# Image 1's queries and offset convolution between image 0's gathers

## The chip, the cores and the metric

The kernel runs on one core of one Trainium2 chip. The metric is the device time of one execution in microseconds (us); smaller is better. The core's engines are called PE (matrix products), DVE, ACT and POOL (work on vectors), and SP (only transfers); each takes its instructions from its own queue in order, and DMA transfers run beside them, issued by SP, ACT or POOL. "PE clock" is the share of full speed granted to PE, as the profile records it.

## The reference

Four layers stand one after another, each `x = x + f(gn(x))`, where `gn` is a group norm of 32 groups; x is [4, 32, 32, 384] in float32. Layer 0, a deformable attention of six heads, is what matters here (B images, n = 1024 pixels, G = 6 groups of GC = 64 channels):

```python
q = jnp.einsum('bhwc,cd->bhwd', x, w_q) + b_q
o = lax.conv_general_dilated(q, w_off0, ..., feature_group_count=G) + b_off0   # 3x3
o = layer_norm(o) * ln_g + ln_b;  o = gelu(o)
offset = tanh(einsum(o per group, w_offp)) * [H/2, W/2]
pos = offset + ref                                   # where each pixel of each group samples
xs = _bilinear_sample(xg, pos)                       # four neighbours of pos, weighed
k = xs @ w_k + b_k;  v = xs @ w_v + b_v
attn = softmax(q k^T * scale + _bilinear_sample(rpe, (ref - pos) / 2))
out = (attn @ v) @ w_out + b_out
```

Layer 1 is a grouped attention with 12 heads of 32 channels, which begins with the products `x @ Wg` and `x @ Wqkv`; layer 2 is a normalised box sum; layer 3 is a local attention over 3 x 3 patches.

## The kernel before

**Two lanes.** `Front` computes layer 0 of an image and `Trunk` its layers 1 to 3. The trunk of image b needs the output of front b. Image 0's front therefore runs alone, `layer0(0)`, some 520 us. From then on `layer3` steps the trunk of image b as a generator, and after each step it draws steps of the fronts of images 1 to 3 (`self.fronts`) until the share of front work that has been issued is ahead of the trunk's by LEAD: `TRUNK_STEPS, FRONT_STEPS, LEAD = 1109.0, 714.0, 0.1`. The numbers that a generator yields are its estimates of the work. The order in which the program issues instructions is the order on each engine's queue but for a scheduler, which may move an instruction ahead of others that it doesn't depend on; `keep_in_program_order` (called `pin`) forbids that for the instructions given to it. Tiles come from pools; a tile with a tag and `bufs` buffers waits, at the next use of a buffer, until the readers of its last use are done. A pool has a side, left or right, and goes out of use at the end of its scope; the next pool takes the memory.

**Layer 0 of one image.** Channels are kept in KC = 3 tiles of P = 128 partitions, pixels in NJ = 8 tiles.

- `normed(b)` loads the image in eight pieces (a<-in_x), transposes it to channels on partitions (PE, L589), writes it to DRAM (`x0`), and takes the group norm: `stats` (two bn_stats and a bn_aggr for each third, L324), a mean over groups by a product with `gmat` (L358), and one scaling for each third (L382). It then transposes the result back (L612), copies it to a tile `xn` with ACT (L624), and stores each piece twice to the DRAM table `pairs` (L626, SP), from which the gathers read. For image 1 `xn` has two buffers.
- `inputs0(b)`: queries, for each of the three output tiles one `dense_t` of six 128 x 512 matmuls in float32, which a trace shows as two records each (L403), put into the zero-framed `qpad` by ACT and stored to `q0` by SP (L660). Then the offset convolution, 36 matmuls of 64 x 64 for each of three tiles (L676), evicted by ACT to `oT` (L684). Transposes (L697) and copies (L701) bring it to pixels on partitions. The layer norm, GELU, and `positions` (L500 to L569: sampling positions, bilinear weights `w4`, pixel indices `sidx` and window indices `widx`) run in two halves for image 0.
- Gathers: for each pixel tile j six indirect DMAs issued by POOL (L748, `gat`, three buffers), 48 in all. `weigh(j)` multiplies and adds them on DVE (L761 to L764) to a tile `xs` of the tag `xn` (two buffers), `turn(j)` transposes that on PE (L775) and copies it with ACT (L780) to `xsT`, and for image 0 `value(j)` makes six matmuls of 128 x 384 (L417) and an addition on DVE (L792). The loop issues gather(j+2), turn(j-1), weigh(j), value(j-2). When all are done, the keys follow (18 matmuls through `dense_t`, L403; L818, L819).
- Heads: `heads0` for image 0 works through 96 blocks of 128 x 512 in a software pipeline of its own. POOL gathers a window of the position bias (L999, L1131, from `strips`), `z` and `lg` are made by DVE and ACT, PE adds the bias by a product with diagonal matrices `dg` (L1052, L1058) and multiplies by keys and values. `outputs0` is the output projection, with the residual, to DRAM (`x1`).

**What image 0's front does for image 1.** In the heads of image 0, `early0` runs `normed(1)` in small steps, one between blocks. The normalised image 1 goes to DRAM (`xh1`, L636). In image 1's own `inputs0`, the first thing that the trunk's first loop draws from `self.fronts`, it is loaded again by ACT's queue (L645, a<-xh) and the queries and convolution follow.

**Start of the trunk.** `start()` (L1190) loads image 0's x1 in three chunks (whole<-x) on SP, takes the norm (L324, L358, L382), and its first product is Wg (L403, big<-whole), then Wqkv.

Of the kernel before, what the change touches and what calls it, by code (L numbers as in the profile page):

```python
# [26 lines left out]
P = 128  # L27
# [34 lines left out]
TRUNK_STEPS, FRONT_STEPS, LEAD = 1109.0, 714.0, 0.1  # L62
# [10 lines left out]
class Net:  # L73
# [135 lines left out]
    def scratch(self):  # L209

        self.pairs = []
        for i in range(2):
            t = self.dram.tile([G * SLOTS, 2 * GC], F32, tag=f"pairs{i}", name=f"pairs{i}")
            self.pairs.append(t)
        dram = lambda name, shape: self.dram.tile(shape, F32, tag=name, name=name)

        self.x0 = [dram(f"x0_{i}", [C, N]) for i in range(2)]
        self.x1 = [dram(f"x1_{i}", [C, N]) for i in range(2)]

        self.qd, self.kd, self.xgd, self.yd = (dram(n, [C, N]) for n in ("qd", "kd", "xgd", "yd"))  # L220

        self.xh1 = dram("xh1", [C, N])
        self.q0, self.k0 = dram("q0", [C, N]), dram("k0", [C, N])
        self.gcd = dram("gcd", [C, M1])
        self.vd = dram("vd", [N, C])

        self.nd, self.rnd = dram("nd", [NH1, N + M1]), dram("rnd", [NH1, N + M1])

        self.den = [dram(f"den{h}", [1, N]) for h in range(G)]
        self.rden = [dram(f"rden{h}", [1, N]) for h in range(G)]  # L230
        self.lse = [dram(f"lse{p}", [2, N]) for p in range(NH1 // 2)]
        self.skew = [
            self.dram.tile([NJ, P * ROWP], F32, tag=f"skew{i}", name=f"skew{i}")
            for i in range(2)
        ]
# [39 lines left out]
    def layer0(self, b):  # L275

        if b == 0:
            for _ in self.front.layer0(b):
                pass
            self.done = self.ahead = 0.0  # L280
            self.fronts = (w for i in range(1, NB) for w in self.front.layer0(i))
# [7 lines left out]
    def layer3(self, b, out):  # L289

        for w in self.trunk.image(b, out):
            self.done += w / TRUNK_STEPS
            while self.ahead < self.done + LEAD:
                self.ahead += next(self.fronts, FRONT_STEPS) / FRONT_STEPS
        assert self.ahead >= min(b + 1, NB - 1)
# [130 lines left out]
class Front(Lane):  # L426


    def layer0(self, b):
        nc, v = self.nc, self.nc.vector  # L430
        with self.scope("l0"):
            self.qpad = self.wt([P, KC, PW, PW], "qpad")
            nc.gpsimd.memset(self.qpad, 0.0)
# [8 lines left out]
            if b == 0:  # L442

                self.side = "left"
                with self.scope("l0f"):
                    self.side = "right"
                    self.heads = self.heads0(self.work)
                    with self.scope("l0a"):
                        yield from self.inputs0(b)
                    yield from self.heads  # L450
                    self.side = "left"
                    yield from self.outputs0(b)
                    self.side = "right"
                return
# [35 lines left out]
    def positions(self, oall, js, tmp, w4, sidx):  # L490
# [37 lines left out]
        floor(fl, qc, HW)  # L528
        v.tensor_tensor(al, q, fl, ALU.subtract)
# [12 lines left out]
        fi = self.wt([P, len(js), G], "ix_fi")  # L542
        fi2 = fi.rearrange("p j g -> p (j g)")

        def index(out, hi, lo, mul, which):
            v.scalar_tensor_tensor(fi2, hi, float(mul), lo, ALU.mult, ALU.add)
            v.tensor_tensor(fi, fi, bc(self.gofs[:, which, :], 1, len(js)), ALU.add)
            v.tensor_copy(out, fi2)

        index(sidx[:, cols], fl[:, 1, :], fl[:, 0, :], HW, 0)  # L550

# [78 lines left out]
    def early0(self):  # L632

        with self.scope("l0p"):
            xh = yield from self.normed(1)
            self.nc.sync.dma_start(self.xh1.rearrange("(k p) n -> p k n", p=P), xh)  # L636

    def inputs0(self, b):
        nc, v = self.nc, self.nc.vector
        pairs = self.pairs[b % 2]  # L640
        if b == 1:

            xh = self.wt([P, KC, N], "a12", 2)
            for k in range(KC):
                nc.scalar.dma_start(xh[:, k], self.xh1[k * P : (k + 1) * P, :])  # L645
            yield 25
        else:
            xh = yield from self.normed(b)
        yield 10
        qpad = self.qpad  # L650
        w = self.weights("w_q")
        for ko in range(KC):
            ps = self.dense_t(w, xh, ko)
            nc.scalar.activation(
                qpad[:, ko, 1 : 1 + HW, 1 : 1 + HW],
                ps.rearrange("p (y x) -> p y x", y=HW),
                AF.Identity,
                bias=self.col(C_BQ, ko),
            )
            nc.sync.dma_start(  # L660
                self.q0[ko * P : (ko + 1) * P, :].rearrange("c (y x) -> c y x", y=HW),
                qpad[:, ko, 1 : 1 + HW, 1 : 1 + HW],
            )
            yield 5


        oT = self.wt([P, KC, 2, N // 2], "a12", 2)
        for k in range(KC):
            ps = self.big().rearrange("p (g n) -> p g n", g=2)
            woff = self.conv_weights(k)  # L670
            for t in range(9):
                dy, dx = divmod(t, 3)
                for h in range(2):
                    for g in range(2):
                        ch = slice(GC * g, GC * (g + 1))
                        nc.tensor.matmul(  # L676
                            ps[GC * h : GC * (h + 1), g, :],
                            woff[ch, t, ch],
                            qpad[ch, k, dy + 16 * h : dy + 16 * h + 16, dx : dx + HW],
                            start=t == 0,  # L680
                            stop=t == 8,
                        )
            for g in range(2):
                nc.scalar.activation(  # L684
                    oT[:, k, g, :], ps[:, g, :], AF.Identity, bias=self.boff[:, k, g : g + 1]
                )
            yield 15
        if b == 0:
            self.cut()
# [16 lines left out]

        parts = 2 if b == 0 else 1
# [4 lines left out]
        for part in range(parts):  # L712
            js = range(size * part, size * (part + 1))
            for j in js:
                st = self.wt([P, 6], "ln_st", 2)
                v.bn_stats(st, oall[:, j, :])
                v.bn_aggr(mv[:, j, :], st)
            rstd = self.wt([P, size], "ln_rstd", 2)
            nc.scalar.activation(
                rstd,  # L720
                mv[:, js.start : js.stop, 1:2].rearrange("p j o -> p (j o)"),
                AF.Sqrt,
                bias=self.eps[:, 1:2],
            )
            v.reciprocal(rstd, rstd)
            for i, j in enumerate(js):
                o = oall[:, j, :]
                v.scalar_tensor_tensor(
                    o, o, mv[:, j, 0:1], self.rows[:, R_LNG : R_LNG + C], ALU.subtract, ALU.mult
                )  # L730
                v.scalar_tensor_tensor(
                    o, o, rstd[:, i : i + 1], self.rows[:, R_LNB : R_LNB + C], ALU.mult, ALU.add
                )
            for j in js:
                nc.scalar.activation(oall[:, j, :], oall[:, j, :], AF.Gelu)
            yield 25 / parts
            self.positions(oall, js, tmp, w4, sidx)
            yield 20 / parts
# [5 lines left out]
        def gather(j):  # L744
            gat = self.wt([P, G, 2, 2 * GC], "gat", 3)
            for g in range(G):

                nc.gpsimd.indirect_dma_start(  # L748
                    out=gat[:, g].rearrange("p l c -> p (l c)"),
                    out_offset=None,  # L750
                    in_=pairs[:, :],
                    in_offset=bass.IndirectOffsetOnAxis(
                        ap=sidx[:, j * G + g : j * G + g + 1], axis=0
                    ),
                )
            return gat

        def weigh(j, gat):
# [5 lines left out]
            v.tensor_tensor(  # L764
# [4 lines left out]
            )  # L769
            return xs  # L770
# [15 lines left out]
        gats, xss = {0: gather(0), 1: gather(1)}, {}  # L786
# [13 lines left out]
        for j in range(NJ + 1):  # L800
# [4 lines left out]
            if j < NJ:  # L805
                xss[j] = weigh(j, gats.pop(j))
            if b == 0 and j > 1:
                value(j - 2)
            if j > 0:
                yield 7  # L810
        if b == 0:

# [129 lines left out]
    def heads0(self, work):  # L942
# [13 lines left out]

        def tile_of(shape, tag, bufs):
            return work.tile(shape, F32, tag=tag, name=self.nm(tag), bufs=bufs)
# [31 lines left out]
        def turn(t):  # L990
# [5 lines left out]
            if i + 5 < n:  # L996
                h, q, j = blocks[i + 5]
                win[i + 5] = tile_of([P, (HH + 1) * WROW], "win", 6)
                nc.gpsimd.indirect_dma_start(  # L999
# [6 lines left out]
                )  # L1006
# [120 lines left out]

        for i in range(4):
            h, q, j = blocks[i]
            win[i] = tile_of([P, (HH + 1) * WROW], "win", 6)  # L1130
            nc.gpsimd.indirect_dma_start(  # L1131
# [6 lines left out]
            )  # L1138
# [5 lines left out]
        other = self.early0()  # L1144
        for t in range(-3, n + OUT + 12):
            turn(t)
            if t > 2 * NJ:
                next(other, None)
        yield 0

    def over_sums(self, k):
# [20 lines left out]
        yield 2  # L1172

# [836 lines left out]
```

## Time and profile before

| What | us |
|---|---|
| runs shown, before (three) | 4414.36, 4414.2, 4400.94 |
| median of them | 4414.2 |
| the profiled execution, its own time | 4398.5 |
| its span, first to last instruction | 4396.7 |
| PE busy in the span | 3905.3 (89%), granted clock 0.949 |
| DVE busy | 3107.1 (71%) |
| ACT busy | 2307.2 (52%) |
| POOL busy | 955.4 (22%) |

The durations come from the profiled execution, whose time includes 1.8 us beside the span (4398.5 - 4396.7). The busy shares are means over a front in which one image is alone and a trunk in which two generators share the engines, so the front is best read by its stretches. Image 0's front, by the trace: normed, queries and convolution from 0 to 78 us; layer norm and positions to 107; gathers, weighing and values to 177; keys to 199; heads to 480; output projection to 517; the trunk's first product is at 573.5.

### The profile page before, as it was taken

The page shows a single profiled execution, that of the slowest core. Times are in us where ns is not written, and L with a number is a line of the kernel's source. Part 1 is how long each engine was busy: PE and PEld are TensorE (multiplying, and loading weights), DVE is VectorE, ACT ScalarE, POOL GpSimd, SP SyncE. Part 2 cuts the span into 40 slices and gives each one's busy share as a digit, 9 for nine tenths or more (in the row PEclk, how much of TensorE's full clock was granted, in tenths as well). Part 3 has the DMA queues.
Part 4 walks back from the last instruction along what each step waited for, and adds up shares of the span by engine and source line. Part 5 has one row for each costly group of instructions (what it writes and reads, how often), then busy time and mean ns, then how long its engine had stood idle before and what let it go on. Part 6 is the DMA issues. An engine that isn't in the chain of part 4 may idle for free.

```text
span 4396.7 us, 45258 instructions
## 1 busy us (share of the span) xinstructions
PE 3905.3 (89%) x14792; PEld 1673.4 (38%) x14792; DVE 3107.1 (71%) x5897; ACT 2307.2 (52%) x3641; POOL 955.4 (22%) x975
## 2 busy tenths in 40 slices
PE   5588889998999898999899989888989998999998
PEld 2233334333334343333333444343333344344444
DVE  4599565888887638687878754768787874566654
ACT  2177343766665324566666433456675741566633
POOL 0655223212212104211212010522121311000000
PEclk8799989999999998999999999899999999999999
DMA  7445244222212255312322135432121213311111
GB/s 149 161 148 146 94 123 139 86 59 75 68 54 68 74 159 164 106 53 56 88 59 85 39 100 159 146 110 67 46 86 41 84 36 128 115 34 34 32 33 43
DMA packets 299052, 389.73 MB, mean 89 GB/s; under 512 B 168694, under 2 KB 230402, under 8 KB 298818
## 3 DMA queue, kind: packets, MB, share of 16 engines
q1 hardware_dynamic: 246130, 220.14, 18.1%
q0 software_dynamic: 39936, 145.53, 10.9%
q10 hardware_dynamic: 12752, 21.19, 1.5%
q8 instruction: 117, 1.92, 0.2%
q14 instruction: 117, 0.96, 0.1%
HBM read 300.48 MB, written 86.56 MB: 88 GB/s over the span
## 4 chain that ended last, share of the span: by engine, by line
PE 49%; DVE 24%; issue 9%; ACT 9%; POOL 4%; DMA 4%; SPq 0%; ACTq 0%; DVEq 0%; POOLq 0%
PE bank L1586 10%; PE big L1556 6%; PE big L403 5%; DVE nmax L1430 4%; DVE e L1593 3%; PE bank L925 3%; ACT big L1431 3%; PE bank L417 3%; PE big L1421 3%; POOL gat L748 3%; PE bank L1581 2%; PE big L676 2%; PE bank L1259 2%; PE bank L1528 2%; PE bank L890 2%
## 5 line engine op out<-in xcount | busy, mean ns | idle before, releaser
L1586 PE MATMUL bank<-whole,sg 128*128 128x512 f32 (+3 forms) x2304 | 850.4, 500 | 2.1 <-POOL sg L1539 0.6
L1593 DVE SCALAR_TENSOR_TENSOR e<-bank,gam,e 128x512 f32<-128x512 f32 x768 | 560.3, 747 | 294.9 <-PE bank L1586 175.5
L1431 ACT ACTIVATE big<-big,nmax 128x1024 f32<-128x1024 f32 x384 | 417.4, 1087 | 295.9 <-DVE nmax L1430 295.8
L1586 PEld LDWEIGHTS bank<-whole,sg 128*128 128x128 f32 x2304 | 399.5, 196 | 348.0 <-issue 269.7
L1556 PE MATMUL big<-qa,ka 64*128 64x512 f32 x1536 | 445.2, 661 | 87.1 <-ACT big L1431 83.6
L1430 DVE TENSOR_REDUCE nmax<-big 128x1 f32<-128x1024 f32 x384 | 452.7, 1218 | 60.7 <-PE big L1421 60.5
L1564 ACT ACTIVATE e<-big 128x1024 f32<-128x1024 f32 x384 | 381.7, 1019 | 172.8 <-PE big L1556 162.0
L866 POOL DMA_INDIRECT win<-strips,widx x288 | 313.6, 1089 | 692.1 <-DVE z L879 377.5
L1539 POOL TENSOR_SCALAR sg<-whole,gam 128x512 f32<-128x512 f32 x192 | 150.2, 782 | 1336.3 <-PE bank L1586 1070.0
L1421 PE MATMUL big<-k,q 32*128 32x512 f32 x1536 | 270.1, 655 | 46.2 <-ACT big L1431 33.7
L748 POOL DMA_INDIRECT gat<-pairs,sidx x192 | 211.0, 1099 | 363.9 <-DVE ix_gt L520 212.2
L925 PE MATMUL bank<-lg,va 128*128 128x512 f32 x576 | 267.3, 605 | 14.7 <-ACT lg L924 14.7
L1556 PEld LDWEIGHTS big<-qa,ka 64*128 64x128 f32 x1536 | 145.8, 196 | 344.7 <-ACT big L1431 178.6
L884 DVE SCALAR_TENSOR_TENSOR lg<-z,bias_f,lg 128x512 f32<-128x512 f32 x288 | 216.2, 768 | 47.4 <-ACT lg L883 45.6
L878 ACT ACTIVATE z<-win,bias_f 128x528 f32<-128x528 f32 x288 | 205.3, 736 | 56.1 <-DVE lg L884 26.2
L923 DVE TENSOR_TENSOR lg<-lg,tb 128x512 f32<-128x512 f32 x288 | 182.2, 691 | 73.0 <-ACT tb L916 73.0
L879 DVE SCALAR_TENSOR_TENSOR z<-win,bias_f,z 128x528 f32<-128x528 f32 x288 | 215.5, 765 | 20.0 <-ACT z L878 18.4
L1528 PE MATMUL bank<-e,vs 128*32 128x512 f32 x1536 | 212.0, 621 | 17.1 <-DVE vs L1522 17.1
L1598 ACT COPY gn<-bank 128x128 f32<-128x128 f32 (+2 forms) x288 | 106.1, 369 | 204.9 <-DVE e L1593 203.9
L883 ACT ACTIVATE lg<-z,bias_f 128x512 f32<-128x512 f32 x288 | 199.7, 716 | 15.3 <-DVE z L879 12.4
L893 DVE TENSOR_TENSOR lg<-bank,lg 128x512 f32<-128x512 f32 x288 | 191.4, 683 | 12.2 <-PE bank L890 11.4
L890 PE MATMUL bank<-qs,kz 64*128 64x512 f32 x288 | 169.0, 671 | 13.4 <-DVE e L1593 8.3
(311 smaller groups left out, 6297.7 us busy)
## 6 DMA issues: line engine op xcount, KB each, us to landing
q<-qd SPq DMA_DIRECT2D x48, 256.0 KB
xg<-xgd SPq DMA_DIRECT2D x48, 256.0 KB
w<-in_gmat SPq DMA_DIRECT2D x16, 576.0 KB
pairs<-gat SPq DMA_DIRECT2D x48, 192.0 KB
w<-in_w_off SPq DMA_DIRECT2D x12, 576.0 KB
w<-in_Wqkv SPq DMA_DIRECT2D x12, 576.0 KB
a<-in_x SPq DMA_DIRECT2D x16, 384.0 KB
x<-a ACTq DMA_DIRECT2D x4, 1536.0 KB
```

What stands on the lines that cost most here:

```text
L748: nc.gpsimd.indirect_dma_start(out=gat[:, g].rearrange("p l c -> p (l c)"), out_offset=None, in_=pairs[:, :], in_offset=bass.IndirectOffse ...
L866: nc.gpsimd.indirect_dma_start(out=win, out_offset=None, in_=self.strips[:, :], in_offset=bass.IndirectOffsetOnAxis(ap=self.widx[:, q, c : ...
L890: nc.tensor.matmul(ps[u], w, mov, start=True, stop=True)
L925: nc.tensor.matmul(po, self.values_of(h, j), lf, start=j == 0, stop=j == NJ - 1)
L1421: nc.tensor.matmul(ps[r][:, h * 512 : (h + 1) * 512], self.q4[rows, i * P : (i + 1) * P], self.k4[rows, 0:512], start=True, stop=True,)
L1430: v.tensor_reduce(nmax[:, r, i : i + 1], ps[r], AX.X, ALU.max, negate=True)
L1431: nc.scalar.activation(ps[r], ps[r], AF.Exp, bias=nmax[:, r, i : i + 1], accum_out=den[:, r, i : i + 1],)
L1528: nc.tensor.matmul(av[r0 : r0 + HD1, :], vs[:, r, :], es[h][:, r, :], start=j == 0, stop=j == NJ - 1,)
L1556: nc.tensor.matmul(ps[:, r, :], ka[rows, j * P : (j + 1) * P], qa[rows, cols], start=True, stop=True,)
L1564: nc.scalar.activation(e, ps, AF.Exp)
L1586: last = nc.tensor.matmul(ps[:, (mid - i0) * P :], sg[:, r, m, :], sim[:, h, r, m, (mid - i0) * P :], start=m == 0, stop=m == 1,)
L1593: v.scalar_tensor_tensor(e[:, r, :], ps, self.gam[:, 1:2], e[:, r, :], ALU.add, ALU.mult, accum_out=tot[:, r, h : h + 1],)
```

## The change

Image 1's queries and offset convolution are computed by a new generator, `Early`, between the parts of image 0's `inputs0`, ahead of image 0's heads, together with image 1's `normed`. `EARLY = (12, 0, 14, 8, 8)` says how many of its steps are taken: 12 ahead of image 0's layer norm, none after its first half, 14 after its second half, 8 in the first round of the loop over gathers and 8 in each later round; what is left runs ahead of the keys. `early0` goes. The padded queries (`qp1`, 1.78 MB) and the convolution (`of1`, 1.57 MB) of image 1 go to DRAM in place of `xh1` (1.57 MB), and image 1's `inputs0` loads them instead of computing them; it still stores `q0` for its heads. Image 1 needs no memset of `qpad` there. Early's weights are in a pool of their own with two buffers.

Beside that: the gathers and the windows' gathers are pinned to the program's order; each `weigh` is kept behind the one before (`issue_after`); the first half of image 0's layer norm and positions is issued with high priority; `positions` computes the pixel index `sidx` ahead of the bilinear weights and not after them (all images); the pools of `heads0` are split in two (`l0f` for win, z and dg, `l0g` for the rest), and the second, with the first four windows, is opened after the inputs, where Early's memory has come free. The windows' first four gathers are thus issued after all 48 gathers. FRONT_STEPS becomes one number for each image, all 714 as before.

```diff
-TRUNK_STEPS, FRONT_STEPS, LEAD = 1109.0, 714.0, 0.1
+EARLY = (12, 0, 14, 8, 8)
+TRUNK_STEPS, FRONT_STEPS, LEAD = 1109.0, (714.0, 714.0, 714.0), 0.1
...
+                    self.heads = self.heads0(room)
+                    next(self.heads)
+                    self.early = Early(self.net, "left").begin(b + 1)
                     with self.scope("l0a"):
                         yield from self.inputs0(b)
                     yield from self.heads
...
+        index(sidx[:, cols], fl[:, 1, :], fl[:, 0, :], HW, 0)
         v.tensor_tensor(al, q, fl, ALU.subtract)
...
         if b == 1:
-            xh = self.wt([P, KC, N], "a12", 2)
-            for k in range(KC):
-                nc.scalar.dma_start(xh[:, k], self.xh1[k * P : (k + 1) * P, :])
-            yield 25
+            nc.sync.dma_start(qpad.rearrange("p k y x -> p (k y x)"), self.qp1)
+            oT = self.wt([P, KC, 2, N // 2], "a12", 2)
+            nc.scalar.dma_start(oT.rearrange("p k g n -> p (k g n)"), self.of1)
+            yield 95
...
+        for _ in range(EARLY[0]):
+            next(ahead, None)
         parts = 2 if b == 0 else 1
...
+                if b == 0 and part == 0:
+                    stack.enter_context(self.tc.high_priority())
...
+            for _ in range(EARLY[1 + part]):
+                next(ahead, None)
...
-                nc.gpsimd.indirect_dma_start(
+                pin(nc.gpsimd.indirect_dma_start(
...
-                xss[j] = weigh(j, gats.pop(j))
+                with ExitStack() as stack:
+                    if weighed:
+                        stack.enter_context(self.tc.issue_after(weighed[-1]))
+                    xss[j] = weigh(j, gats.pop(j))
             if b == 0 and j > 1:
                 value(j - 2)
+            for _ in range(EARLY[-2 + (j > 0)]):
+                next(ahead, None)
...
+            for _ in ahead:
+                pass
             next(self.heads)
...
-        other = self.early0()
         for t in range(-3, n + OUT + 12):
             turn(t)
-            if t > 2 * NJ:
-                next(other, None)
...
+class Early(Front):
+    def weights(self, name, lo=0):
+        return Net.weights(self, name, lo)
+    def conv_weights(self, k):
+        return self.taps[k] if k in self.taps else Net.conv_weights(self, k)
+    def norm_steps(self, x, out):
+        gmat, self.wq = self.weights("gmat"), self.weights("w_q")
+        yield from super().norm_steps(x, out, None, gmat)
+        self.taps = {}
+        self.taps[0] = self.conv_weights(0)
+    def begin(self, b):
+        nc = self.nc
+        with self.scope("l0p"), self.tc.tile_pool(
+            name=self.nm("l0w"), bufs=2, side=self.side
+        ) as self.wts:
+            self.qpad = self.wt([P, KC, PW, PW], "qpad")
+            nc.gpsimd.memset(self.qpad, 0.0)
+            xh = yield from self.normed(b)
+            for ko in range(KC):
+                self.project(xh, ko, self.wq)
+                yield
+            self.taps[1] = self.conv_weights(1)
+            oT = self.wt([P, KC, 2, N // 2], "a12", 2)
+            for k in range(KC):
+                yield from self.convolve(oT, k)
+            nc.sync.dma_start(self.qp1, self.qpad.rearrange("p k y x -> p (k y x)"))
+            nc.sync.dma_start(self.of1, oT.rearrange("p k g n -> p (k g n)"))
```

`project` and `convolve` are the loops of `inputs0` for the queries and the convolution, taken out into functions; `convolve` yields after each tap (9 for each tile).

## The prediction

> **What bounds the kernel now.** I read the page first (PE busy 89% of the span, but about half in the first two of its 40 slices), then busy time by stretches of the first 760 us, then the timeline of the places where PE idles, then the chain of waits there. The change touches only image 0's solo front and the start of the trunk.
>
> First the solo front, busy time by stretches (columns: stretch, then busy us and instructions of each engine, granted clock, DMA share, GB/s):
>
> ```profile
> core 0: us, PE busy (x) PEld busy (x) DVE busy (x) ACT busy (x) POOL busy (x), PEclk, DMA share, GB/s
> 90.00:95.00 5.00, 0.00 (x0) 0.00 (x0) 5.00 (x7) 1.20 (x3) 0.00 (x0) 0.50 0.00 0
> 160.00:170.00 10.00, 5.81 (x12) 3.38 (x13) 4.29 (x5) 0.48 (x1) 7.73 (x8) 0.66 0.33 97
> 240.00:260.00 20.00, 18.59 (x51) 7.28 (x51) 19.93 (x27) 14.98 (x25) 11.10 (x12) 1.00 0.34 101
> 340.00:360.00 20.00, 16.91 (x54) 7.03 (x54) 17.45 (x26) 11.87 (x23) 9.53 (x10) 1.00 0.90 246
> 520.00:530.00 10.00, 1.87 (x3) 0.81 (x4) 4.05 (x11) 1.28 (x1) 0.16 (x2) 0.54 0.90 322
> ```
>
> Layer norm and positions (78 to 107) are DVE alone. The gathers (107 to 177) are POOL's: one issue every 1.25 us, PE half idle. The heads (199 to 480) are DVE's, at 19.9 of 20 us, except in 340 to 380, where image 1's early work makes ACT wait for its stores (6.8 us in two waits, below) and DVE idles 2.55 and 1.49 us.
>
> Then the hand-over to the trunk: the timeline of PE, the transfers and DVE, the chain of waits (start, us, what), and the longest wait of that early work in 240 to 370.
>
> ```profile
> 186.68 10.46 PE L403 MATMUL big<-a,w 128*128 128x512 f32 x24
> 198.92 1.45 PE L1052 MATMUL big<-z,dg 128*128 128x512 f32 x3
> ...
> 528.13 2.04 PE L403 MATMUL big<-a,w 128*128 128x512 f32 x2 [11.14 <-DMA a<-xh]
> 529.97 2.99 PE L358 MATMUL bank<-gn_mv,w 128*128 128x2 f32 x14
> 532.82 17.38 PE L403 MATMUL big<-a,w 128*128 128x512 f32 x34
> 550.13 23.41 PE L676 MATMUL big<-qpad,w 64*64 64x512 f32 x216
> ```
> ```profile
> 522.40 0.32 SPq L1190 DMA_DIRECT2D whole<-x  x1
> 522.62 1.31 ACTq L645 DMA_DIRECT2D a<-xh  x3
> 527.67 1.29 DVE L324 BATCH_NORM_STATS2 gn_st<-whole 128x6 f32<-128x512 f32 x2 [5.38 <-DMA whole<-x]
> 534.12 2.26 DVE L382 TENSOR_SCALAR whole<-whole,gn_mean,gn_rstd 128x1024 f32<-128x1024 f32 x3
> ```
> ```profile
> 550.20 23.34 PE big L676 x216
> 573.54 10.50 PE big L403 x24
> ```
> ```profile
> ACT xn L624 <- DMA pairs<-xn: 6.8, 2, 5.1
> ```
>
> This is the heart of the case. The trunk's input is normalised by 536.4 (534.12 + 2.26), but its first product, Wg at 573.5, stands in PE's queue behind image 1's queries (to 550) and offset convolution (to 573.5). DVE and ACT, idle from 536 to 580 but for evictions, wait with it. The chain of waits runs through all of it.
>
> **The change, part by part.** By the compiled order of the instructions on each engine (which has no times), from Wg on, PE's order is the same to the end; DVE's and POOL's differ by neighbours changing places.
>
> Trunk start. Leave the 18 query and 108 convolution matmuls out, and Wg waits for its own input: statistics done, mean product L358, 534.12 the scaling, PE at about 535.2. That is 573.5 - 535.2 = 38.3 us less. Two things take some back.
> (a) In the after, SP issues the load of the padded queries (1.78 MB) ahead of the trunk's last input chunk (0.52 MB), and ACT the convolution's load (1.57 MB) beside it, where before the weights (0.59) and xh (1.57) ran. At the 322 GB/s of the row 520 to 530, split evenly between the two queues from 522.6: some 1 MB of queries left plus the chunk is 1.5 MB at 160 GB/s, 9.4 us, so it lands near 533 and not 527.7: +5.5. Bounds: 0 if the chunk gets through at once, +8 if all is served first (3.9 MB, 12 us, behind 2 us of latency that both have).
> (b) A cold clock: 36 query pieces took 2.04 + 17.38 = 19.4 us at 0.54 and 0.60, Wg's 24 10.57 at 1.00, so 15.9 for 36: the start cost 3.5, and Wg now pays it. Bounds 2 to 5.
> By the Trainium skill ("TensorE: Matmul & The Clock Gate", Part 1: The HAM clock gate), PE runs at half rate after an idle window of some 3.4 us and until a busy one has passed; by that the cold start would lose 1.7 us a window, and (b) would be 1.7 to 3.4. The trace's 0.50 at idle agrees.
> The query stores (3, of 2.9 us of SP each at 48 us) now stand together on SP at about 531 to 540, ahead of the second Wqkv weights; PE needs those 24 us after Wg begins, so 10 us and more of cover. ACT loses 3 x 1.12 + 6 x 0.63 = 7 us here, off the path: nothing. Sum: -38.3 + 5.5 + 3.5 = -29.3.
>
> Heads. Out go 6 bn_stats (3.98 us), 3 aggregates (0.59), 3 scalings (2.85) and 5 small DVE rows (0.16 each): 8.2 us of an engine that is full, and the 3.9 us that it idled in 340 to 380. I take -11 (bounds -8, if other waits fill the idle, and -13). PE's 55 and ACT's 16 smaller pieces are not on the path.
>
> Layer norm, ahead of the first gather. The same statistics (3.98 + 0.59 + 0.65 for four small rows) now lie in DVE's full stretch: +5.2; the mean product, 3.1 us on PE, is covered by about 2 us of L500 and casts: +1.2; some seven of image 1's first transposes (2.80 us for 12) precede the first eviction that DVE needs: +1.6; about 8 small rows of 0.1 us move behind the pixel index: -0.8. First gather at 114.6, not 107.4. SP and DMA: image 1's weights and first chunk (1.6 MB) go out before SP's stores to pairs, in 25 to 35 us where the DMA share is 0.48 and 0.41; nothing, and up to +5 if the third convolution weights, for which PE already waits 2.97 us at 65.7, land later. The strips, pushed behind three loads, are due only at the windows, which POOL now issues 40 us later.
>
> Gathers and keys, by two paths. POOL: 52 issues (four of them windows) took 107.4 to 177.0, 1.34 us each; now 48, so the last leaves at 114.6 + 64.3 = 178.9; the windows after it still precede the z that waits for the last turn. With the 21.9 us that lay between last gather and L1052, and 14 key matmuls instead of 12 behind the last turn (+1.7), that path ends at 202.5. PE: from the first scaled third of image 1 (about 119) until L1052 it must now do image 1's last 24 transposes (0.27 each, 6.5), queries (15.9 warm, see (b)) and convolution (23.4) beside its own turns (24 at 0.27, 6.5), values (8 at 2.10) and keys (36 pieces, 10.46 for 24: 15.7): 84.8 us, so 203.8; with one cold start of 3.5 and about 1 us for the second convolution weights, which SP sends behind image 1's stores, 208.3. PE is the later: it becomes the bound of this stretch, and image 0's values and turns, which stand in its queue behind image 1's work, and DVE's next weigh behind each value, come late by 4 to 7 us on the way. I take 208.3, +9.4 on 198.9. Bounds: +3.6 (POOL's path) and +25 (PE cold in half of its new work). The stores of image 1 go through two buffers; eight copies took 331.8 to 358.5, 27 us, and here some 30 lie open. The two last stores (3.35 MB, 10 us at 322) go out by 180, under the keys; the heads' tiles that reuse that memory are first written near 190.
>
> Images 1 to 3: their pixel index is written about 1 us earlier and the chain passes through POOL's gathers after 629; I take -1.5 in all (0 to -3). Pinning the gathers leaves their order: nothing.
>
> Total: -29.3 - 11 + 9.4 - 1.5 = -32 us. Against the profiled execution's own 4398.5 that is 4366, against the median of the runs shown, 4414.2, it is 4382. Two of the three runs lie at the median and one, at 4400.9, with the profile, so I take 4411 for the kernel before and give 4379. All low ends together make -36.3 - 13 + 3.6 - 3 = -49, all high ones -25.3 - 8 + 25 + 0 = -8: the forecast's own range is 4350 (-49 on 4398.5, were the next runs like the profile) to 4403 (-8 on 4411), and 4408 with the 5 us of the convolution weights.
>
> **A rule that speaks against it.** The row is the chunk's 5.27 us from issue (522.40) to use. By the Trainium skill ("DMA: Bandwidth & Descriptors", Queues, rings and completion order) each DMA engine goes round-robin over the queue rows, and within one row descriptors start in ring order, so a small load behind a large one on SP waits for it; that is what (a) prices, and without it the sum would be 5.5 us lower. The row cannot tell the two queues apart.
>
> **Rivals.**
> 1. The opened gap is refilled: Wg does not go when its input lands, or what follows (image 1's norm and taps share DVE, full in 590 to 620; its gathers are on the chain at 630) has a limit that does not move with Wg. For it: PE idles 12 us in 620 to 660 even now. Against: all of that follows Wg or loads that now come earlier. Then only heads and front count, -11 + 9.4, and a fifth of the trunk's 29 (-6): -8, 4403.
> 2. Slower: image 1's stores choke the gathers. ACT's third copy waits for the stores of its first; image 0's turns stand behind it on ACT and PE, the last convolution weights behind on SP, and DVE's weighs behind value. The forecast has some 30 us for the eight copies; each us beyond lengthens the stretch by one. That eats the gain at 30 + 32 = 62 us, and at 90 us the kernel is 28 us slower, 4439. For it: 5.1 us in one such wait, and strips, weights and gathers share the DMA. Against: 0.33 DMA share and 97 GB/s in the gathers.
> 3. The change does not do what it says: excluded, the compiled order has the matmuls between the gathers.
>
> **How the numbers follow.** Forecast 0.79, rival 1 0.11, rival 2 0.10. A measurement of this kernel tells about 0.3% (13 us) from no change. The forecast is faster but for its high end, 0.06 of the 0.79; rival 1's -8 is no change, with 0.03 of its 0.11 beyond the border. So faster 0.76, same 0.06 + 0.08 = 0.14, slower 0.10, all rival 2. The range 4350 to 4408 holds the forecast with its bounds and rival 1 at its middle, and leaves out rival 2 and the tails.
>
> **What would show it.** In the profile after: first gather at 113 to 117; PE's first L1052 near 208; DVE at 19.9 of 20 in every stretch of the heads, which end some 2 us sooner than before (-11 + 9.4); no L676 between the output projection and Wg; Wg 27 us behind the projection's end (535.2 - 516.9, and 5.5 + 3.5), not 57. It would be wrong if value or turn waits push the last gather past 195, if Wg waits for something other than the input chunk, or if the shift at 600 us is gone at 1600.

## The result, and the profile after

| | before | changed |
|---|---|---|
| median (7 runs each) | 4408.83 us (4400.94 to 4418.42) | 4372.89 us (4362.77 to 4388.01) |
| profiled execution, span | 4396.7 us | 4368.5 us |

The ratio of the changed kernel to the one before is 0.992, 95% interval 0.990 to 0.9939: 27 to 44 us faster. The forecast was 4379, range 4350 to 4408. A second series gave 0.9914 (0.9893 to 0.9934), so about 36 us.

First busy time by stretches, the places shown of before (columns as there):

```profile
core 0: us, PE busy (x) PEld busy (x) DVE busy (x) ACT busy (x) POOL busy (x), PEclk, DMA share, GB/s
160.00:170.00 10.00, 10.00 (x85) 3.93 (x81) 4.91 (x6) 1.74 (x3) 7.87 (x8) 1.00 0.34 105
340.00:360.00 20.00, 16.16 (x43) 5.74 (x42) 19.90 (x30) 14.29 (x24) 9.67 (x12) 1.00 0.46 137
520.00:530.00 10.00, 3.15 (x14) 3.06 (x14) 2.15 (x8) 0.00 (x0) 0.00 (x0) 0.50 1.06 264
```

Between the gathers PE went from 5.81 of 10 us to 10.00. In 340 to 360, DVE is full (19.90, was 17.45) and the DMA share is 0.46, not 0.90: image 1's stores are gone from the heads. In 520 to 530 PE and ACT do nothing but the mean product: the trunk waits for a transfer. Then PE's timeline at the two ends of the heads (L407 is L403 of before, L362 is L358, L1083 is L1052; L797 turns a weighed tile, L775 of before):

```profile
183.06 0.52 PE L797 MATMUL bank<-ident,xn 128*128 128x128 f32 x3 [1.83 <-DVE xn L785]
185.35 12.18 PE L407 MATMUL big<-a,w 128*128 128x512 f32 x28
197.37 2.10 PE L421 MATMUL bank<-w,a 128*128 128x384 f32 x6
199.30 1.02 PE L1083 MATMUL big<-z,dg 128*128 128x512 f32 x2
...
498.50 9.53 PE L407 MATMUL big<-qpad,w 128*128 128x512 f32 x19
526.42 3.15 PE L362 MATMUL bank<-gn_mv,w 128*128 128x2 f32 x14 [18.39 <-DVE gn_mv L358]
531.69 12.18 PE L407 MATMUL big<-whole,w 128*128 128x512 f32 x24 [2.12 <-DVE whole L386]
```

The last products of the projection before were these:

```profile
506.26 10.72 PE L403 MATMUL big<-qpad,w 128*128 128x512 f32 x20 [4.05 <-DVE qpad L988]
```

The heads begin at 199.30 (198.92 before), the output projection ends at 508.03 (498.50 + 9.53; 516.98 before), and Wg starts at 531.69 (573.5), waiting for its own scaled input and for nothing of image 1. Ahead of the last turn (183.06) PE still waits 1.83 us for the last weighed tile: PE is nearly full between the gathers, and the gathers still set when the heads begin. The chain of waits at the hand-over names what is late now:

```profile
510.82 2.94 DMA x<-res
...
513.78 10.64 DMA whole<-x
...
531.69 12.18 PE big L407 x24
```

The last input chunk takes 10.64 us from issue to use, where it took 5.27. The timeline of SP, ACT and DVE shows the load of the padded queries just ahead of it:

```profile
510.82 0.32 SPq L495 DMA_DIRECT2D x<-res  x1
511.52 0.32 SPq L675 DMA_DIRECT2D qpad<-qp  x1
513.78 0.32 SPq L1254 DMA_DIRECT2D whole<-x  x1
513.83 0.35 ACTq L677 DMA_DIRECT2D a<-of  x1
524.44 1.28 DVE L328 BATCH_NORM_STATS2 gn_st<-whole 128x6 f32<-128x512 f32 x2 [10.82 <-DMA whole<-x]
```
The waits of ACT for image 1's stores, now between the gathers, were not long:

```profile
ACT xn L628 <- DMA pairs<-xn: 4.0, 2, 3.4
```

Matching the two traces' instructions from the end, the changed kernel is 0.4 us late at the start of the heads, 10 us early at 400 and 41 us early at 700. It stays within 3 us of 41 until 2700 and is 30 us early from 3700 on. What this last piece is, experiment 9 shows.

### The profile page after: what moved, and what is told of

Read it like the earlier page. It is cut to its first block, busy times and chain, and to the rows that moved or that the text cites. A ratio compares the mean times of both kernels' runs of the same rounds, so it can differ in the third digit from the quotient of the medians.

```text
span 4368.5 us, 45247 instructions
## 1 busy us (share of the span) xinstructions
PE 3897.6 (89%) x14792; PEld 1670.5 (38%) x14792; DVE 3106.5 (71%) x5897; ACT 2306.7 (53%) x3640; POOL 962.5 (22%) x975
## 4 chain that ended last, share of the span: by engine, by line
PE 49%; DVE 25%; issue 9%; ACT 8%; POOL 4%; DMA 4%; SPq 0%; ACTq 0%; DVEq 0%; POOLq 0%
PE bank L1650 10%; PE big L1620 6%; PE big L407 4%; DVE nmax L1494 4%; PE bank L953 4%; DVE e L1657 3%; ACT big L1495 3%; PE bank L421 3%; POOL gat L769 3%; PE big L1485 3%; PE bank L1645 2%; PE bank L1323 2%; PE bank L1592 2%; DVE z L907 2%; DVE lg L912 2%
```

## The experiments

Where the text gives a hand-over, it is the time from the end of image 0's output projection to Wg; "heads" is from the first L1052 (L1083) to that end. Each ratio is to the kernel before, run beside it on the same chip.

**1. The norm alone.** Early keeps `normed`; queries and convolution go back to the trunk's start.

```diff
             xh = yield from self.normed(b)
-            for ko in range(KC):
-                self.project(xh, ko, self.wq)
-                yield
...
-            nc.sync.dma_start(self.of1, oT.rearrange("p k g n -> p (k g n)"))
+            nc.sync.dma_start(self.xh1.rearrange("(k p) n -> p k n", p=P), xh)
```

> The changed kernel, but Early computes only image 1's normed (with its stores to pairs) between image 0's inputs, and stores the normalised image; image 1's queries and convolution are computed at the start of the trunk as in the kernel before. If the gain is a sum of two separate pieces, this has the heads' piece alone: the heads (first L1052-type product to end of the output projection) take 309 us and not 318, the hand-over (end of projection to Wg) is 56 to 57 us as before, first heads product at 195 to 200, total 7 to 13 us below the kernel before. Rival: the piece at the heads comes from the reordering of pools and pins, or normed beside the gathers costs what it gives: total 0 to -3 us.

```profile
200.72 1.45 PE L1075 MATMUL big<-z,dg 128*128 128x512 f32 x3
500.83 10.30 PE L406 MATMUL big<-qpad,w 128*128 128x512 f32 x20 [5.30 <-DVE qpad L1011]
567.05 3.27 PE L406 MATMUL big<-whole,w 128*128 128x512 f32 x7
```

The ratio is 0.9979 (0.9964 to 0.9994), 9 us with 3 to 16 possible. The heads take 310.4 us (200.72 to 511.13), not 318, and the hand-over is 55.9, as before. So the sum has two pieces that can be taken apart: heads 8 us, hand-over the rest. The heads began at 200.72, which lies among the starts of the executions that have the convolution there (199.3 to 203.7 in five, below), although 39 us of PE work were missing: that work costs nothing that shows where it was put. The pinned gathers and the split pools are in every kernel with Early; no run has them alone, so what they give by themselves is not shown.

**2. The same work behind Wg.** The kernel before, with image 1's queries and convolution drawn after Wg.

```diff
                 nc.scalar.dma_start(xh[:, k], self.xh1[k * P : (k + 1) * P, :])
-            yield 25
+            yield 97
...
-            yield 5
+            yield 0 if b == 1 else 5
...
-            yield 15
+            yield 0 if b == 1 else 15
```

> The kernel before, with image 1's queries and convolution drawn only after Wg has been issued (its first estimate is 97 and not 25 + 10, the following ones 0, and a later one 2 less so that the pace behind is the same). Theory 'place': the 39 us of PE work are free between the gathers, where PE was idle, but not in the trunk, where PE is busy 168 of 186 us; so Wg starts 33 to 38 us earlier, image 1's block then stands behind it, and only what DVE and ACT do beside the block is won: total -4 to -14 us. Rival 'order': the gain at the hand-over was only that Wg waited in line, and the work itself finds room later: total -28 to -38 us. Third: image 1's gathers, which come later by Wg's 10 us, are on the chain: total +5 to +12.

The ratio is 0.9999 (0.998 to 1.0018), that is no change, with 9 us less to 8 us more possible. PE's timeline of this kernel:

```profile
535.86 18.34 PE L403 MATMUL big<-whole,w 128*128 128x512 f32 x36 [2.12 <-DVE whole L382]
554.03 15.61 PE L403 MATMUL big<-a,w 128*128 128x512 f32 x36
569.58 23.41 PE L676 MATMUL big<-qpad,w 64*64 64x512 f32 x216
592.92 0.66 PE L697 MATMUL big<-ident,a 128*128 128x128 f32 x4
```

Wg starts at 535.86, 38 us earlier than in the kernel before, and the 39 us behind it (15.61 and 23.41) give all of it back: at 700 us the trace is 1 to 3 us late. Nothing of the expected -4 to -14 is seen, though the interval leaves room for its upper part and for some of the third expectation's +5 to +12; "order" (-28 to -38) is excluded. Starting Wg earlier is worth nothing measurable by itself. It pays in the changed kernel because PE's work went to a place where PE was idle.

**3. More work in that place.** Image 1's query products made twice in Early.

```diff
                 self.project(xh, ko, self.wq)
+                self.dense_t(self.wq, xh, ko)
```

> The changed kernel with image 1's three query products computed twice in Early (18 matmuls of 128x512 more, results of the second unused): 15.7 us more of PE work between the gathers. Theory: PE bounds the stretch from 113 to 199: first heads product 12 to 16 us later (211 to 215), total +12 to +16 against the changed kernel. Rival: POOL's gathers bound it (last at 176.7) and PE still has room: first heads product +0 to +5, total the same.

The heads start at 206.35, 7.05 us behind the changed kernel's 199.30 and 3 to 7 behind the five starts named above, between the two expectations; the ratio is 0.9938 (0.9919 to 0.9956) against 0.992, which agrees with 7 us but doesn't settle it. Busy time from 113 us to the heads, of before, of the changed kernel and of this one:

```profile
113.00:199.00 86.00, 45.78 (x109) 23.70 (x110) 39.11 (x60) 7.08 (x13) 56.46 (x53) 0.73 0.38 118
```
```profile
113.00:199.00 86.00, 80.81 (x384) 37.24 (x385) 42.02 (x79) 17.31 (x30) 61.23 (x54) 0.95 0.75 228
```
```profile
113.00:206.00 93.00, 93.00 (x418) 42.90 (x417) 41.38 (x79) 17.42 (x30) 60.47 (x54) 0.98 0.70 209
```

```profile
190.13 0.49 PE L797 MATMUL bank<-ident,xn 128*128 128x128 f32 x3
```

PE had 40.2 us idle before and has 5.2 now; with the double queries it has none, and its last turn (190.13, the line just above) waits for nothing, where the changed kernel's waited 1.83 us for the last weighed tile. So PE becomes the bound only here. The changed kernel leaves the place nearly full, and of the 15.7 us added beyond it 3 to 7 lengthen the front.

**4. Where the chunk waits: another queue.** The load of the queries issued by ACT.

```diff
-            nc.sync.dma_start(qpad.rearrange("p k y x -> p (k y x)"), self.qp1)
             oT = self.wt([P, KC, 2, N // 2], "a12", 2)
             nc.scalar.dma_start(oT.rearrange("p k g n -> p (k g n)"), self.of1)
+            nc.scalar.dma_start(qpad.rearrange("p k y x -> p (k y x)"), self.qp1)
```

> The changed kernel with the load of the padded queries (1.78 MB) issued by ACT, with the convolution's, and not by SP ahead of the trunk's last input chunk. If the chunk waits behind the queries in SP's own ring, it is used 5 to 6 us after its issue and not 10.7: Wg 4 to 6 us earlier, total -4 to -6 against the changed kernel, unless image 1's transposes, whose input comes later, cost it. If transfers share the engines whatever the queue, the chunk still takes 10 to 11 us: no change.

Neither size came. The ratio is 0.9907 (0.9882 to 0.9931), as the changed kernel's, and the hand-over is 25.0 us, 1.3 longer. Its timeline of transfers, and DVE's first use of the chunk:

```profile
509.91 0.35 ACTq L677 DMA_DIRECT2D qpad<-qp  x1
512.51 0.32 SPq L495 DMA_DIRECT2D x<-res  x1
519.92 0.32 SPq L1254 DMA_DIRECT2D whole<-x  x1
519.97 0.35 ACTq L676 DMA_DIRECT2D a<-of  x1
527.61 1.29 DVE L328 BATCH_NORM_STATS2 gn_st<-whole 128x6 f32<-128x512 f32 x2 [12.30 <-DMA whole<-x]
```

On ACT's queue the 1.78 MB go out at 509.91, ahead of the last residual's store, and that store, on SP's queue, now takes 7.41 us (512.51 to 519.92) and not 2.94. The chunk, issued only when it has landed, is used at 527.61, 7.7 us later, with the convolution's load issued beside it. A queue of its own did not shield the small transfer.

**5. Where the chunk waits: later loads.** Both loads on SP, kept in order behind the chunk.

```diff
-            nc.sync.dma_start(qpad.rearrange("p k y x -> p (k y x)"), self.qp1)
             oT = self.wt([P, KC, 2, N // 2], "a12", 2)
-            nc.scalar.dma_start(oT.rearrange("p k g n -> p (k g n)"), self.of1)
+            pin = self.tc.keep_in_program_order
+            pin(nc.sync.dma_start(oT.rearrange("p k g n -> p (k g n)"), self.of1))
+            pin(nc.sync.dma_start(qpad.rearrange("p k y x -> p (k y x)"), self.qp1))
...
-            self.nc.sync.dma_start(x[:, k, :], self.x1[b % 2][k * P : (k + 1) * P, :])
+            t = self.nc.sync.dma_start(x[:, k, :], self.x1[b % 2][k * P : (k + 1) * P, :])
+            if b == 0:
+                self.tc.keep_in_program_order(t)
```

> The changed kernel with both loads of image 1 (convolution, then queries) on SP, kept in SP's order behind the trunk's last input chunk. With the load of the queries on ACT the last residual's store took 7.4 us instead of 3, and the chunk came no sooner: the transfers share the bandwidth, whatever the queue. If that is the cause, putting both loads behind the chunk makes store and chunk as quick as in the kernel before (chunk used 5.3 us after its issue, not 10.7): Wg 5 to 6 us earlier, at 525 to 527, hand-over 18 to 19 us, not 23.7; image 1's transposes are then due 2 to 6 us after Wg's second product and may take back up to 4. Total -2 to -6 against the changed kernel. Rival: the chunk waits for something else at that place: no change in Wg.

> The kernel of e_load_late once more, on the same chip as the changed kernel. Its hand-over was 16.8 us, not 23.7, but 13 us were lost between 620 and 660 to waits that the profile puts down to no release. If that loss was of that execution alone, it is gone here, and the kernel is 3 to 7 us faster than the changed kernel; if it comes from the later loads, it is there again, and the kernel is the same or up to 8 us slower.

The hand-over is 16.8 us in the first, 17.0 in the second, and 23.7 and 23.8 in two executions of the changed kernel: the chunk is late because the two large loads run while it does. Which of the two does it, and how much the order within one queue adds, is not separated. The timeline of the second:

```profile
512.49 0.32 SPq L495 DMA_DIRECT2D x<-res  x1
515.46 0.32 SPq L1255 DMA_DIRECT2D whole<-x  x1
515.83 0.42 SPq L677 DMA_DIRECT2D a<-of  x1
519.21 1.28 DVE L328 BATCH_NORM_STATS2 gn_st<-whole 128x6 f32<-128x512 f32 x2 [3.90 <-DMA whole<-x]
526.45 11.93 PE L407 MATMUL big<-whole,w 128*128 128x512 f32 x24 [2.12 <-DVE whole L386]
```

The store takes 2.97 us and the chunk 3.75. The first run's loss between 620 and 660 us is not there in the second (PE idle 3.8 us from 600 to 665). What it is worth in all stays open: the ratios are 0.9901 (0.9879 to 0.9923) and 0.9906 (0.9884 to 0.9927), beside 0.9914 of the changed kernel in the series of the second. The median there is 8.5 us lower (4368.1 against 4376.6), within the spread.

**6. The heads: work or waits.** The kernel before, with four `xn` buffers for image 1.

```diff
-                xn = self.wt([P, C], "xn", 2)
+                xn = self.wt([P, C], "xn", 4)
```

> The kernel before with four buffers, not two, for the tiles from which image 1's normalised pieces are stored in image 0's heads, so that ACT waits less for the stores. The heads' piece of the gain (318.0 us before, 308.7 after) is 8.2 us of DVE work and at most 3.9 us of DVE's idle. Theory 'work': only the idle goes, heads 314 to 317, total -1 to -4. Rival 'waits': the gain was ACT's waits of 12 us (6.8 + 5.1), the work fits beside: heads 308 to 311, total -7 to -10.

```profile
340.00:360.00 20.00, 19.56 (x56) 7.17 (x55) 19.90 (x30) 15.40 (x28) 10.34 (x11) 1.00 0.86 229
360.00:380.00 20.00, 16.66 (x44) 6.20 (x44) 19.93 (x29) 13.79 (x23) 9.93 (x12) 1.00 0.41 117
```

The heads take 314.7 us (195.86 to 510.54), and DVE is full where it idled (19.90 and 19.93 of 20 us, with ACT's waits for the stores gone): some 3.3 of the 8 to 9 us was ACT's wait. DVE's busy time from the heads to the projection's end is 288.42 us here, 287.98 before and 281.37 with the change, so the rest agrees with DVE's work, as "work" said. The ratio, 0.9983 (0.9967 to 1.0), doesn't tell the two apart: its middle, -7.5 us, is nearer the rival's sum, and its interval holds both.

**7. Image 1's steps behind the layer norm.**

```diff
-EARLY = (12, 0, 14, 8, 8)
+EARLY = (0, 0, 26, 8, 8)
```

> The changed kernel with EARLY = (0, 0, 26, 8, 8): none of image 1's steps ahead of image 0's layer norm, all after its positions. If image 1's norm on DVE is what moved the first gather from 107.4 to 108.6, the first gather is at 104 to 107.5; but PE gets image 1's first transposes and queries later (first scaled third after 113), and since PE had only 5.2 us idle from 113 to 199, the heads start 3 to 10 us later (202 to 209): total +3 to +10. Rival: POOL's gathers bound the stretch, and the heads follow the first gather: -1 to -4.

This failed as a test: the scheduler still put image 1's transposes (72 us) and its statistics (75 us) where they were, so the first gather stayed at 108.04. Its heads began at 211.90, but not for the theory's reason: PE's timeline has

```profile
156.34 6.89 PE L656 MATMUL big<-qpad,w 64*64 64x512 f32 x26
164.05 1.83 PE L656 MATMUL big<-qpad,w 64*64 64x512 f32 x3 [0.82 <-issue]
166.17 2.56 PE L656 MATMUL big<-qpad,w 64*64 64x512 f32 x3 [0.29 <-issue]
```

That is 32 records in 12.4 us, where the changed kernel has 64 in 7.10, and no release is named for the waits. The ratio is 0.9896 (0.987 to 0.9923), no slower than the changed kernel's, so this seems to belong to that one execution; the kernel was traced once. Where the first gather's delay comes from, the kept traces show all the same. The layer norm's first statistic and the first gather, before, and with the change (there with DVE's wait for image 1's mean product):

```profile
77.62 0.56 DVE L716 BATCH_NORM_STATS2 ln_st<-a 128x6 f32<-128x384 f32 x1 [46.02 <-ACT a L701]
107.40 1.16 POOL L748 DMA_INDIRECT gat<-pairs,sidx  x1 [93.85 <-DVE ix_pos L506]
```
```profile
75.32 0.54 DVE L735 BATCH_NORM_STATS2 ln_st<-a 128x6 f32<-128x384 f32 x1
102.05 0.16 DVE L372 TENSOR_SCALAR gn_mean<-bank 128x3 f32<-128x3 f32 x1 [1.38 <-PE bank L362]
108.56 1.22 POOL L769 DMA_INDIRECT gat<-pairs,sidx  x1 [71.89 <-DVE ix_pos L514]
```

The stretch between the two takes 29.78 us before and 33.24 with the change. It hardly differs between executions: 29.77 and 29.78 in experiments 2 and 6, whose front is that of before, and 33.23 or 33.24 in the changed kernel's second execution and in experiments 1, 3, 4 and 5 (33.35 in this one). So the change adds 3.5 us here, whatever the time at which the layer norm begins.

**8. The pixel index.** The edit alone on the kernel before (twice), and the changed kernel without it.

```diff
         floor(fl, qc, HW)
...
+        index(sidx[:, cols], fl[:, 1, :], fl[:, 0, :], HW, 0)
         v.tensor_tensor(al, q, fl, ALU.subtract)
...
-        index(sidx[:, cols], fl[:, 1, :], fl[:, 0, :], HW, 0)
```

> The kernel before with one edit of the change alone: positions computes the pixel index ahead of the bilinear weights, for all images. The first gather comes about 1 us earlier (106.2 to 106.6, not 107.4); heads begin 0 to 1 us earlier; for images 1 to 3 nothing or -1 us each: total 0 to -3, not to be told from no change. Rival: the edit is worth several us through the three other images' gathers: total -5 or more.

> The kernel of e_index_first once more (the kernel before with the pixel index first). Its median was 0.36% under that of before, 14 us, though its first gather and its heads stand where those of e_xn_heads stand. By the prediction's sizes: 0 to -3 us. If the edit is worth 0.36%: -10 to -20 us.

> The changed kernel with the pixel index computed behind the bilinear weights, as in the kernel before. By the prediction's sizes the first gather comes 0.5 to 1 us later, and the whole is 0 to 3 us slower than the changed kernel. If the edit is worth what the median of e_index_first said (0.36%), it is 10 to 20 us slower.

The first series gave 0.9964 (0.9948 to 0.998), the second 0.9992 (0.9982 to 1.0002). Without the edit the changed kernel has 0.9922 (0.9903 to 0.9941) beside 0.9914. In the total this can't be told from no change, as predicted; the first series' 14 us did not come again, which shows how far one series of a few runs can lie off. The stretch of experiment 7 does show the edit: 28.95 and 28.94 us with it on the kernel before (29.78 without), and 34.05 without it in the changed kernel (33.24 with it). The index is worth 0.8 us ahead of image 0's first gather, and image 1's norm costs 4.3.

**9. The changed kernel once more.**

> The changed kernel, unchanged, as the base for the three runs beside it and for its own profile. By the runs so far: ratio 0.990 to 0.994 to the kernel before. The two profiles that were compared differ by 41 us from Wg to 2700 us and by 30 us behind 3700 us; the profiles of two other kernels lose 12 to 14 us against the profile of before in the same stretch, so this drift should be one of that profile and not of the change: against the first profile of the changed kernel this one should move by steps of 1 to 2 us with no fixed place. If the drift belongs to the change, the loss from 2700 to 3700 is there again against the profile of before and is absent in the kernels of e_index_first.

The ratio is 0.9914 (0.9893 to 0.9934). Its heads began at 201.82, and its hand-over was 23.8. The piece that the first pair of profiles loses from 2700 to 3700 (41 to 30 us) is also lost against the profile of before by the kernels of experiments 1 (14 us) and 2 (13 us), over the same stretch and with very different starts; here the lead falls from 40 to 25. The two executions of the kernel of experiment 8 that has the index first, in which the expectation looked for no loss if the change were its cause, lose 22 and 10 us there. So that profile of before (4398.5, under all seven runs shown of it) was quick in that stretch, and nothing in it is laid to the change.

## Why the prediction was right, step by step

- **Trunk start, -29.3: right in mechanism and size.** The hand-over fell from 56.5 to 23.7, -32.8 (foreseen -38.3 + 5.5 = -32.8), and Wg's 24 pieces took 12.18 and not 10.57 us, +1.6 for the cold clock (foreseen 3.5): -31.2. Step (a) had the right +5.4 with a reason that only half held: it split the bandwidth between queues and put the chunk behind the rest of the queries. Experiment 4 showed that another queue does not save the chunk, experiment 5 that another time does. With the rule cited there (the Trainium skill, "DMA: Bandwidth & Descriptors", Queues, rings and completion order) the runs agree in the round-robin over the rows: two rows share the engines, 7.41 us for a store that takes 2.94. That the wait came from one row's ring order they do not show. For (b), the estimate worked out from the Trainium skill ("TensorE: Matmul & The Clock Gate", Part 1: The HAM clock gate) was 1.7 to 3.4; the measured 1.6 lies just under it, and other executions with image 1's convolution in Early paid 1.4 to 3.0 (11.93 to 13.54 us for the 24 pieces).
- **Heads, -11: right cause, too large.** The heads took 9.3 us less in the pair and about 8 less over the other executions (310 against 318 us). DVE lost 6.6 us of busy time, not 8.2, and 2 to 3 us of its idle.
- **Layer norm, +7.2: too dear.** In the pair of profiles the first gather moved by 1.2 us, but the layer norm of before began late there (77.62 us, 74.4 to 75.9 in four other traces with its front), its last convolution tile having taken 9.65 us and not 7.96 as in those. From the first statistic to the first gather the change costs 3.5 us (experiment 7): 4.3 for image 1's rows and mean product, where 6.4 were foreseen (+5.2 + 1.2), less the 0.8 that the index gives, as foreseen. The wait for the mean product was 1.38 us, so the term that was too large is the statistics' +5.2: the first of six (74.71) ran ahead of the layer norm, and neighbouring rows start 0.60 us apart where the sum took 0.66 for each. The term "+1.6 for image 1's first transposes" failed: the layer norm begins at 74.4 to 75.8 with Early, no later than without. The bound of +5 for later convolution weights did not come either: PE's wait for them, 2.97 us before, is 0.6 to 1.8.
- **Gathers and keys, +9.4: wrong bound.** The step that failed is "PE is the later: it becomes the bound". PE was nearly full (80.81 of 86 us busy), but ahead of the last turn it waited 1.83 us for the last weighed tile (4.24 in the changed kernel's second execution), so POOL's gathers still set the end: the heads began 21.7 us behind the end of the last gather (177.60), and the prediction's POOL path had 21.9 there. PE became the bound only with the 15.7 us more of experiment 3. PE's row began at 112.94 and not at 119, and 84.8 us from there end at 197.7. The cold start did come, with a granted clock of 0.50 from 112 to 118 us, and the second convolution weights cost PE 3.36 us, not 1; both fitted into PE's slack. The heads began at 199.30, +0.4; in five executions (two of the changed kernel, one of experiment 4, two of experiment 5) at 199.3 to 203.7, against 194.6 to 198.9 in five of kernels without Early, so +4 at the middle, near the low bound of +3.6. That is the later first gather: from the first gather to the heads the five take 90.7 to 95.5 us (median 91.1), those without Early 89.8 to 92.6 (median 91.5).
- **Index, -1.5: nothing measurable in the total**, as its bounds allowed.
- **The sum.** In the pair it is +0.4 - 9.3 - 31.2 = -40, and by the other executions' middle +4 - 8 - 31 = -35, which is what the medians show. The forecast's -32 came from two terms too dear (+9.4, and -29.3 by 2) and two too good (-11 and -1.5), which nearly cancel in the middle figure. That they do is luck; that the trunk start is by far the largest term, and was right, is not.
- **The signs.** DVE full in the heads, no L676 ahead of Wg, and a shift that is still there at 1600 us came as named. The first gather at 113 to 117 (108.56) and the first heads product near 208 (199.30) did not, and the heads ended 9 us sooner than before, not 2. Wg stood 23.7 us behind the projection's end and not 27: the 3.5 us of cold clock in that 27 are paid inside Wg, not ahead of it.
- **Rivals.** 1, the gap refilled, did not come: the lead was 41 us at 700 and at 2700. Experiment 2 is what it would have looked like. 2 did not come: ACT waited 4.0 us for image 1's stores in all, and although the profile puts one wait of 6.0 us of DVE's weighing down to them too, the last gather was at 176.65 (176.07 before).

## What to carry to other kernels

Work that stood ahead of the critical product gained nothing when it was only put behind it: it must go where its engine is idle, and the busy time of that stretch says how much fits (here 40 us of idle took 39 us of work, and the time from the first gather to the heads stayed as it was). Where an input chunk is on the path, the large loads that are not yet needed belong behind it in time, since another queue did not keep them out of its way here. And one profile of before is one execution: landmarks of other kernels that share its front tell how far its own are typical, and the length of a stretch on one engine can show 0.8 us that no total shows.

## What the runs showed of the hardware

- PE's added work partly paid for itself, as the clock stayed up. With the norm alone between the gathers (experiment 1), the granted clock from 113 to 200 was 0.72 and a value product of six pieces took up to 4.05 us; with queries and convolution there, in the first profile of the changed kernel, it was 0.95 and every one took 2.10.
- A load of 1.78 MB on ACT's queue made a 0.52 MB store on SP's queue take 7.41 us instead of 2.94.
- Two executions held stretches in which PE's work came slowly with no release named. In the first of experiment 5 PE was busy 47.31 us of the 65 from 600 on, and 61.14 in the next execution of the same kernel; in experiment 7 32 records took 12.4 us, in a kernel that was traced once.
